# A new order of the steady loop and of both ends in a window-attention and LoRA kernel

## The chip, the cores and the metric

The kernel runs on one core of a Trainium2 chip. The metric is the device time of one execution in microseconds (us), as the median of several runs; lower is better. The core has five engines, each with a queue of its own that it works off in order: PE (matmul, with its weight loads shown as PEld), DVE (vector), ACT (scalar, activation functions), POOL (GpSimd) and SP (here it only issues DMAs). An instruction that has to wait for another engine holds up all that stand behind it in its own queue.

## The reference

The input x has 32 sequences of 512 tokens with 256 features, in float32. For each sequence:

```python
x = x + attn(layernorm(x), wq, wk, wv, wo, q_norm_w, k_norm_w)
x = x + ffn(layernorm(x), weight, gate_w, lora_U, lora_V)
# attn: 16 query heads, 4 key/value heads of 64; rmsnorm on q and k per head;
#   a query sees itself and the 127 tokens before it; softmax; then y @ wo.T
# ffn: gate = softmax(xt @ gate_w.T) over 8 experts; base = xt @ weight.T;
#   t = xt @ lora_U (rank 16); out = base + (1/16) * sum_e gate_e * (t_e @ lora_V_e)
```

## The kernel before

The tokens are cut into tiles of 128, four to a sequence, so N = 128 tiles in all; t is the place of a tile in its sequence. Each tile goes through the same stages, each a small method of the class `Tile`:

- `ln1_stats`, `ln1_eps`, `ln1_rs`, `ln1_neg`: mean and variance of x and the factor 1/sqrt(var + eps) (DVE, ACT, POOL, ACT). `trx` transposes x on DVE (L390).
- `kv_pe` (L398) and `q_pe(0)`, `q_pe(1)` (L413): matmuls to k and v, and to two halves of q. `kv_copy`, `ksq`, `q_copy`, `qsq` read the results on ACT (L404 to L426), `vdiff` reads v on DVE.
- `ksum`, `qsum` (DVE), `q_eps` (ACT), `pow` (POOL, L319), `kn`, `qn` (POOL): the norm of q and k. `trk`, `trq` transpose them in 32x32 blocks on DVE; `move` (L353) lets SP issue 16 DMAs that bring the blocks to their places, together with blocks of the probabilities and of h for other tiles; `kT_copy` reads the keys from there on ACT.
- `s_pe(0)` to `s_pe(3)` (L529): scores of 32 queries each. `s_merge` (L540), `nmaxs` (L545) on DVE, `exps` (L556) on ACT: mask, row maximum, and exponential with its sum, 4 activations for each j. `prob_den`, `prob` (DVE, POOL), `tr` (DVE): division and transposition.
- `pick` (POOL, L599): the part of the probabilities that belongs to the other half of the window. `y_pe` (L627): probabilities times v; its second half, with `other` and `vd`, exists only for t > 0. `y_copy` (ACT, L648), `o_pe` (L654), `o_add` (DVE).
- `ln2_stats`, `ln2_eps`, `ln2_rs`, `trh`, `hT_copy`, `f_pe` (L700), `gmax`, `gexp`, `gmul`, `uT_pe` (L731), `uT_copy`, `lora_pe` (L738), `store`, `put`: the second norm and the feed-forward part, and the result's DMA.

For the first tile of a sequence (t = 0) the first of its score matmuls are narrower (32 to 128 columns instead of 160), `y_pe` has no second half, and `vdiff`, `pick` and `ln1_neg` do nothing; but `s_merge` has a memset more (L539).

The order of the instructions on all five engines is written out by hand, with no scheduler behind it: `slot(i)` is the body of the steady loop and calls each stage once, for the tile that it has reached by then (`at(i - 3).s_pe(0)` is the score stage of the tile three behind i). The calls of one engine make up its queue, in the order in which they stand. The tables `FIRST` and `LAST` are the same kind of list for the first tiles and for the last ones; an entry `q_pe.1:0` is `q_pe(1)` of tile 0, `s_pe.3:-1` is `s_pe(3)` of the last tile.

The results of matmuls lie in PSUM. Four banks, B0 to B3, are shared by all stages except the scores; S0 holds s(0) and s(2), S1 holds s(1) and s(3). A matmul group can begin only when all readers of the previous content of its bank are done. `BANK` says which stage uses which bank in the loop, and `PLACES` gives exceptions, by stage and tile, for the two ends. In SBUF each kind of tile has a fixed number of buffers (`BUFS`), used in turn.

Of the kernel before, what the change touches and what calls it, by code (L numbers as in the profile page):

```python
# [30 lines left out]
def tile_window_attn_lora_ffn(  # L31
# [47 lines left out]
    N = B * NT  # L79
# [28 lines left out]
    for tag, products in {  # L108
        "B0": "tq0 y1 uT",
        "B1": "cqa q0 tq1 y0 o",  # L110
# [9 lines left out]
        ("ckv", 0): "B3",  # L120
        ("cqa", 0): "B2",
        ("cqb", 0): "B0",
        ("q0", 0): "B2",
        ("kv", 0): "B1",
        ("q0", 1): "B3",
        ("q1", 0): "B3",
        ("q0", 2): "B0",
        ("kv", 1): "B0",
        ("cf", 0): "B1",
        ("tq0", 0): "B2",  # L130
        ("tk", 0): "B3",
        ("kv", 2): "B3",
        ("tk", 1): "B0",
        ("tq0", 1): "B3",
        ("tq1", 1): "B3",
        ("q0", 3): "B0",
        ("kv", 3): "B1",
        ("tq0", 2): "B1",
        ("tq1", 2): "B2",
        ("tk", 2): "B1",  # L140
        ("q1", 4): "B0",
        ("q0", 5): "B0",
        ("kv", 5): "B3",
        ("kv", 6): "B0",
        ("y0", 0): "B0",
        ("y1", 0): "B3",
        ("q1", 6): "B3",
        ("y0", 1): "B0",
        ("y1", 1): "B3",
        ("o", 0): "B3",  # L150
        ("o", 1): "B0",
        ("y0", 2): "B3",
        ("y0", 3): "B0",
        ("y1", 3): "B3",
        ("o", 2): "B3",
# [12 lines left out]
        ("y1", -4): "B2",
        ("o", -4): "B3",
        ("f", -7): "B2",  # L170
        ("y0", -3): "B0",
        ("y1", -3): "B3",
        ("hT", -4): "B0",
        ("y0", -2): "B2",
        ("y1", -2): "B1",
        ("uT", -6): "B1",
        ("o", -2): "B2",
        ("hT", -3): "B0",
        ("f", -5): "B1",
        ("y0", -1): "B2",  # L180
        ("y1", -1): "B3",
        ("uT", -5): "B2",
        ("o", -1): "B0",
        ("f", -4): "B0",
        ("uT", -4): "B1",
        ("uT", -3): "B1",
        ("f", -2): "B0",
        ("uT", -2): "B3",
        ("f", -1): "B2",
        ("uT", -1): "B1",  # L190
# [577 lines left out]
    def slot(i):  # L768
        at(i).ln1_stats()
        at(i - 1).q_pe(0)  # L770
        at(i - 11).uT_copy()
        at(i).trx()
        at(i - 4).tr(0)
        at(i).ln1_eps()
        at(i - 1).q_copy(1)
# [181 lines left out]
    with tc.manual_schedule(engines={mybir.EngineType.PE, mybir.EngineType.Activation, mybir.EngineType.DVE, mybir.EngineType.Pool, mybir.EngineType.SP}):  # L957
        in_order(FIRST, 0)
        for i in range(12, N - 1 + 1):
            slot(i)  # L960
# [49 lines left out]
```

## Time and profile before

| what | value |
|---|---|
| median of 3 runs | 2089.67 us (2089.59 to 2089.72) |
| the profiled execution | 2090.21 us |
| its span, first to last instruction | 2088.5 us |
| PE busy | 2071.2 us, 99% |
| DVE busy | 1778.1 us, 85% |
| POOL busy | 1670.9 us, 80% |
| ACT busy | 1530.5 us, 73% |
| granted clock of PE | full over the whole span |
| first matmul starts at | 5.42 us |
| matmuls of wq and x, and of wo | 462.6 us busy (L413), 475.3 us (L654) |
| exponentials on ACT | 720.5 us (L556) |
| DMA | 138 GB/s mean |

The page gives one execution on the chip. A row of PE's timeline gives the start of a group of like matmuls, the time until the modelled end of its last one, the line, the operands and how many instructions it has; each matmul in float32 of the program is two instructions there, a transposition is one. Because the ends overlap with the next group, the distance between two starts is what a group costs. A bracket at the end of a row gives the idle time before it and what ended it.

### The profile page before, as it was taken

Reading aid. Unit: us, or ns where it says so; the run is one execution under the profiler, and the core shown is the slowest. Engines: PE = TensorE matmul, PEld = TensorE weight load, DVE = VectorE, ACT = ScalarE, POOL = GpSimd, SP = SyncE. Lnnn points to the kernel's source line nnn. Section 1 sums busy time; section 2 is a strip of 40 time slices with the busy share of each in tenths; the row PEclk is TensorE's granted clock in tenths of the full one; section 3 lists DMA queues with packets and bytes.
Section 4 is the critical chain, followed back from the end, with each engine's and each line's share of the span. In section 5 each row is a group of like instructions: output and inputs, shape, how many; then the busy total and the mean of one; then the engine's idle time right before and its main releaser. Section 6 shows DMA issues by size and latency. Waiting matters only on the chain.

```text
span 2088.5 us, 43160 instructions
## 1 busy us (share of the span) xinstructions
PE 2071.2 (99%) x12214; PEld 1282.8 (61%) x12214; DVE 1778.1 (85%) x4546; ACT 1530.5 (73%) x6247; POOL 1670.9 (80%) x1291
## 2 busy tenths in 40 slices
PE   8999999999999999999999999999999999999999
PEld 4556666666666666666666666666666666666665
DVE  6988888888888888888888888888898888888884
ACT  6877777777777777777777777777777777777773
POOL 6988778877788788888877887778878888887773
PEclk9999999999999999999999999999999999999999
DMA  5665666566656666665666656665656566656653
GB/s 116 143 154 137 140 144 143 132 140 143 144 133 142 141 140 138 142 144 137 137 142 140 146 134 140 142 146 132 143 136 148 132 143 144 139 135 140 142 130 86
DMA packets 272989, 288.79 MB, mean 138 GB/s; under 512 B 172273, under 2 KB 206705, under 8 KB 272753
## 3 DMA queue, kind: packets, MB, share of 16 engines
q1 hardware_dynamic: 272208, 284.47, 59.6%
q8 instruction: 100, 1.64, 0.4%
q10 hardware_dynamic: 544, 1.57, 0.2%
q14 instruction: 137, 1.11, 0.2%
HBM read 36.71 MB, written 16.78 MB: 26 GB/s over the span
## 4 chain that ended last, share of the span: by engine, by line
PE 89%; ACT 6%; SPq 2%; DVE 1%; DMA 1%; issue 0%; DVEq 0%; ACTq 0%
PE o_ps L654 22%; PE q_ps L413 20%; PE s_ps L529 14%; PE y_ps L627 13%; PE kv_ps L398 11%; PE f_ps L700 6%; ACT ex L556 4%; PE f_ps L738 3%; SPq L353 1%; ACT kv L404 1%; PE uT_ps L731 1%; ACT ksq L408 1%; SPq L238 0%; DVE nmax L545 0%; DMA pT<-tr 0%
## 5 line engine op out<-in xcount | busy, mean ns | idle before, releaser
L556 ACT ACTIVATE ex<-s_ps,nmax 128x128 f32<-128x128 f32 x2048 | 720.5, 387 | 28.5 <-DVE nmax L545 22.3
L319 POOL TENSOR_TENSOR rs<-ss_eps,minus_half 128x20 f32<-128x20 f32 x128 | 453.1, 3539 | 167.1 <-ACT ss_eps L441 165.8
L568 POOL TENSOR_TENSOR ex<-ex,rden 128x1024 f32<-128x1024 f32 x256 | 485.4, 1896 | 96.8 <-DVE rden L564 95.3
L654 PE MATMUL o_ps<-wo_sb,yT 128*128 128x256 f32 x2048 | 475.3, 385 | 0.3 <-ACT yT L648 0.3
L556 ACT ACTIVATION_READ_ACCUMULATOR ex<-s_ps,nmax 128x1 f32 x2048 | 465.9, 228 | 0.0
L413 PE MATMUL q_ps<-wq_sb,xT 128*128 128x512 f32 x1024 | 462.6, 593 | 0.1
L654 PEld LDWEIGHTS o_ps<-wo_sb,yT 128*128 128x128 f32 x2048 | 379.1, 190 | 68.8 <-ACT yT L648 10.6
L545 DVE TENSOR_REDUCE nmax<-s_ps 128x4 f32<-128x512 f32 x512 | 348.6, 681 | 13.0
L529 PE MATMUL s_ps<-kT,pT 64*128 64x160 f32 (+4 forms) x4000 | 335.4, 304 | 3.9 <-ACT ex L556 0.9
L529 PEld LDWEIGHTS s_ps<-kT,pT 64*128 64x128 f32 x4000 | 271.1, 186 | 104.5 <-ACT ex L556 47.0
L599 POOL TENSOR_SCALAR_AFFINE_SELECT other<-pT 64x512 f32<-64x512 f32 x384 | 289.8, 755 | 21.3 <-DMA pT<-tr 5.9
L413 PEld LDWEIGHTS q_ps<-wq_sb,xT 128*128 128x128 f32 x1024 | 184.5, 190 | 192.2 <-issue 173.8
L404 ACT ACTIVATE kv<-kv_ps,ln_rs_a 128x512 f32<-128x512 f32 x128 | 88.3, 690 | 265.0 <-PE kv_ps L398 265.0
L398 PE MATMUL kv_ps<-wkv_sb,xT 128*128 128x512 f32 x512 | 253.5, 617 | 0.6 <-DVE xT L390 0.5
L627 PE MATMUL y_ps<-pT,kv 128*64 128x256 f32 x2048 | 249.3, 385 | 0.0
L458 POOL TENSOR_TENSOR qn<-q,rs 128x1024 f32<-128x1024 f32 x128 | 243.4, 1902 | 0.2
L579 DVE STREAM_TRANSPOSE tr<-ex 128x512 f32<-128x512 f32 (+3 forms) x512 | 240.3, 487 | 2.8 <-DMA pT<-tr 1.1
L421 ACT ACTIVATE q<-q_ps,ln_rs_a 128x512 f32<-128x512 f32 x256 | 176.0, 688 | 51.5 <-PE q_ps L413 50.3
L627 PEld LDWEIGHTS y_ps<-pT,kv 128*64 128x64 f32 x2048 | 135.5, 136 | 125.9 <-ACT ss_eps L441 61.4
L540 DVE COPY_PREDICATED s_ps<-over,s_ps 128x128 f32<-128x128 int32 x512 | 148.4, 290 | 75.4 <-PE s_ps L529 70.8
L700 PE MATMUL f_ps<-wf_sb,hT 128*128 128x392 f32 x512 | 190.1, 494 | 0.1
L426 ACT ACTIVATE qsq<-q_ps,ln_rs_a 128x512 f32<-128x512 f32 x256 | 175.0, 684 | 2.0 <-PE q_ps L413 1.2
(85 smaller groups left out, 2538.3 us busy)
## 6 DMA issues: line engine op xcount, KB each, us to landing
pT<-tr SPq DMA_DIRECT2D x1936, 112.0 KB, 2.3
xb<-in_x_dram SPq DMA_DIRECT2D x256, 64.0 KB, 2.3
x<-in_x_dram SPq DMA_DIRECT2D x128, 128.0 KB, 2.4
out_dram<-res SPq DMA_DIRECT2D x128, 128.0 KB, 2.0
pT<-tr SPq DMA_DIRECT2D x64, 104.0 KB, 2.2
pT<-tr SPq DMA_DIRECT2D x48, 72.0 KB, 2.1
wq_sb<-in_wq_dram ACTq DMA_DIRECT2D x1, 1024.0 KB, 7.4
wo_sb<-in_wo_dram SPq DMA_DIRECT2D x1, 1024.0 KB, 6.5
```

Source lines behind the costliest of these rows:

```text
L319: nc.gpsimd.tensor_tensor(o, v, minus_half[:, : o.shape[-1]], ALU.pow)
L398: nc.tensor.matmul(ps, self.xT[:, c, :], wkv_sb[:, c, :], start=(c == 0), stop=(c == ND - 1))
L413: nc.tensor.matmul(ps, self.xT[:, c, :], wq_sb[:, c, gp * 512 : (gp + 1) * 512], start=(c == 0), stop=(c == ND - 1),)
L458: nc.gpsimd.tensor_tensor(self.q_n.rearrange("p (g d) -> p g d", d=HD), self.q.rearrange("p g (h d) -> p (g h) d", d=HD), self.rs[:, :NH]. ...
L529: nc.tensor.matmul(ps[:, half, gp, o0:n], qT[rows, gp * P : (gp + 1) * P], self.s.kT[rows, gp, k0 + o0 : k0 + n], start=True, stop=True,)
L545: nc.vector.tensor_reduce(self.nmax[j], ps[:, :, :, :P], AX.X, ALU.max, negate=True)
L556: nc.scalar.activation(self.ex[e][:, c, gp, half], ps[:, gp, half, :P], AF.Exp, bias=self.nmax[j][:, gp, half : half + 1], accum_out=self. ...
L568: nc.gpsimd.tensor_tensor(ex, ex, self.rden[e].rearrange("p c g a -> p (c g a)").unsqueeze(2).to_broadcast([P, 8, P]), ALU.mult,)
L599: nc.gpsimd.affine_select(out=self.other[gp][rows].rearrange("p h (c a q) -> p h c a q", c=2, a=2), in_=fr.rearrange("p h (c a q) -> p h c ...
L627: nc.tensor.matmul(ps[e][half * HD : (half + 1) * HD, gp * 4 * H : (gp + 1) * 4 * H], v[:, v0 : v0 + HD], w.rearrange("p h (c a q) -> p a ...
L654: nc.tensor.matmul(ps[:, :D], self.yT[:, c].rearrange("p e t -> p (e t)"), wo_sb[:, c, :], start=(c == 0), stop=(c == NCH - 1),)
L700: nc.tensor.matmul(ps[:, : UG + D], self.hT[:, c, :], wf_sb[:, c, :], start=(c == 0), stop=(c == ND - 1),)
```

## The change

The change rewrites the order and nothing else: the same stages run for the same tiles. It has four parts.

- `slot(i)` has a new order of its calls, and the stages are spread over more tiles: `kv_pe` and `trx` now work on tile i-2 (before: i), `q_pe(0)` and `q_pe(1)` both on i-2 (before: i-1 and i), the scores on i-5 (before: i-3), `tr` on i-6 (before: i-4), `y_pe` on i-8 (before: i-6), `o_pe` on i-9 (before: i-7), `f_pe` on i-12 (before: i-10), `lora_pe` on i-13 (before: i-11). `load_x` and `load_blocks` are called for i+1 and i+3 (before: i+3 and i+5). On PE the order within a slot was q(0), lora, s(0), s(1), kv, f, y, s(2), s(3), o, uT, q(1); it becomes s(0), s(1), kv, lora, y, s(2), s(3), f, q(0), q(1), o, uT.
- `BANK`: o and uT exchange their banks (o to B0, uT to B1).
- `FIRST` and `LAST` are written anew, to lead into this loop and out of it; the loop begins with tile 13 instead of 12.
- `PLACES` is written anew to go with them.

The diff, with the tables cut:

```diff
@@ -106,8 +106,8 @@
 
     BANK = {}
     for tag, products in {
-        "B0": "tq0 y1 uT",
-        "B1": "cqa q0 tq1 y0 o",
+        "B0": "tq0 y1 o",
+        "B1": "cqa q0 tq1 y0 uT",
         "B2": "ckv cqb hT tk kv q1",
         "B3": "cf f",
         "S0": "s0 s2",
@@ -117,77 +117,74 @@
 
 
     PLACES = {
-        ("ckv", 0): "B3",
...
+        ("ckv", 0): "B1",
...
     }
     def slot(i):
+        at(i - 4).trq()
+        at(i - 6).tr(1)
+        at(i - 6).exps(3)
+        at(i - 2).trx()
+        at(i - 3).q_copy(1)
+        at(i - 12).ln2_eps()
+        at(i - 5).s_pe(0)
+        at(i - 3).ksum()
+        at(i - 6).prob_den(1)
+        at(i - 5).s_merge(0)
+        at(i - 5).s_pe(1)
+        at(i - 13).uT_copy()
+        at(i - 8).pick(0)
+        at(i - 5).nmaxs(0)
+        at(i - 8).pick(1)
+        at(i - 10).o_add()
+        at(i - 5).s_merge(1)
+        at(i - 5).nmaxs(1)
+        at(i - 2).kv_pe()
+        at(i - 13).lora_pe()
+        at(i - 8).y_pe()
+        at(i - 5).exps(0)
+        at(i - 5).s_pe(2)
+        at(i - 3).qsum()
+        at(i - 5).exps(1)
+        at(i - 13).store()
+        at(i - 12).ln2_rs()
+        at(i - 10).trh()
+        at(i - 6).tr(0)
+        at(i - 5).prob_den(0)
+        move(i - 7)
+        at(i - 13).put()
+        at(i - 5).s_pe(3)
+        at(i - 6).prob(1)
+        at(i - 5).s_merge(2)
+        at(i - 3).q_eps()
+        at(i - 12).hT_copy()
+        at(i - 8).y_copy(0)
+        at(i - 12).f_pe()
         at(i).ln1_stats()
-        at(i - 1).q_pe(0)
-        at(i - 11).uT_copy()
-        at(i).trx()
-        at(i - 4).tr(0)
+        at(i - 5).nmaxs(2)
+        at(i - 2).kv_copy()
+        at(i - 2).q_pe(0)
+        at(i - 1).ln1_rs()
+        at(i - 1).ln1_neg()
+        at(i - 2).ksq()
+        at(i - 8).y_copy(1)
+        at(i - 2).vdiff()
+        at(i - 2).q_pe(1)
+        at(i - 12).gmax()
+        at(i - 3).pow()
+        at(i - 5).s_merge(3)
+        at(i - 3).kn()
+        at(i - 9).o_pe()
+        at(i - 6).tr(3)
+        at(i - 5).exps(2)
+        at(i - 10).ln2_stats()
+        at(i - 3).trk()
         at(i).ln1_eps()
-        at(i - 1).q_copy(1)
-        at(i - 4).tr(1)
-        at(i).ln1_rs()
-        at(i - 11).lora_pe()
-        at(i - 1).qsq(1)
-        at(i - 4).prob_den(1)
-        at(i - 3).s_pe(0)
-        at(i - 8).ln2_stats()
-        at(i).ln1_neg()
-        at(i - 4).prob(1)
-        at(i - 11).store()
-        at(i - 1).q_copy(0)
-        at(i - 3).s_pe(1)
-        at(i - 11).put()
-        at(i - 1).qsq(0)
-        at(i - 3).s_merge(0)
-        at(i).kv_pe()
-        at(i - 3).nmaxs(0)
-        at(i - 8).ln2_eps()
-        at(i - 1).qsum()
-        at(i - 6).pick(1)
-        at(i - 10).f_pe()
-        at(i - 3).s_merge(1)
-        at(i - 3).nmaxs(1)
-        at(i).kv_copy()
-        at(i - 8).ln2_rs()
-        at(i - 4).tr(2)
-        at(i).ksq()
-        at(i - 6).y_pe()
-        at(i - 1).q_eps()
-        at(i - 3).exps(0)
-        at(i).ksum()
-        at(i - 1).pow()
-        at(i).vdiff()
-        at(i - 3).exps(1)
-        at(i - 4).tr(3)
-        at(i - 10).gmax()
-        at(i - 3).s_pe(2)
-        at(i - 6).y_copy(0)
-        at(i - 3).s_pe(3)
-        at(i - 3).prob_den(0)
-        at(i - 6).y_copy(1)
-        at(i - 3).s_merge(2)
-        at(i - 7).o_pe()
-        at(i - 10).gexp()
-        at(i - 3).nmaxs(2)
-        at(i - 1).kn()
-        at(i - 3).s_merge(3)
-        at(i - 1).qn()
-        at(i - 1).trk()
-        at(i - 3).nmaxs(3)
-        at(i - 2).kT_copy()
-        at(i - 10).gmul()
-        at(i - 3).exps(2)
-        at(i - 3).prob(0)
-        at(i - 1).trq()
-        at(i - 10).uT_pe()
-        at(i).q_pe(1)
-        at(i - 3).exps(3)
-        at(i - 7).o_add()
-        at(i - 5).pick(0)
-        move(i - 4)
-        at(i - 7).trh()
-        at(i - 9).hT_copy()
-        load_x(i + 3)
-        load_blocks(i + 5)
+        at(i - 2).qsq(0)
+        at(i - 5).nmaxs(3)
+        at(i - 12).gexp()
+        at(i - 3).qn()
+        at(i - 2).qsq(1)
+        at(i - 12).gmul()
+        at(i - 2).q_copy(0)
+        at(i - 6).tr(2)
+        at(i - 5).prob(0)
+        at(i - 4).kT_copy()
+        at(i - 12).uT_pe()
+        load_x(i + 1)
+        load_blocks(i + 3)
     FIRST = """
-        ldb:2 ldb:3 mean_kv:0 ldx:0 ln1_stats:0 ldb:0 ldb:1 mean_qa:0 ldx:1 ldx:3 mean_qb:0 sub_kv:0
-        trx:0 ldx:5 ln1_eps:0 trx:1 sub_qa:0 ln1_rs:0 kv_pe:0 kv_copy:0 q_pe.0:0 sub_qb:0 ksq:0
-        qsq.0:0 ldwo:0 q_copy.0:0 ln1_stats:1 ksum:0 ldx:4 ldx:2 ln1_eps:1 ln1_stats:2 ln1_stats:4
-        q_pe.1:0 kv_pe:1 ln1_eps:2 ln1_rs:1 trx:2 ln1_neg:0 ldb:4 ldx:6 ln1_rs:2 q_pe.1:1 ln1_eps:4
...
+        ldb:0 mean_kv:0 sub_kv:0 ldb:2 ldb:1 ldb:3 ldx:1 ldx:0 ldx:2 trx:0 mean_qa:0 ldx:4 mean_qb:0
+        kv_pe:0 sub_qa:0 ldx:3 ldx:5 ln1_stats:0 ln1_eps:0 sub_qb:0 ln1_stats:1 ln1_stats:5 trx:1
+        ln1_rs:0 kv_copy:0 ksq:0 q_pe.0:0 ln1_eps:5 ln1_stats:3 q_pe.1:0 ln1_neg:0 ln1_eps:1 qsq.0:0
+        ln1_eps:3 qsq.1:0 ln1_stats:2 ldx:7 ldb:4 ln1_rs:1 q_copy.0:0 ksum:0 vdiff:0 ln1_eps:2
+        ln1_rs:5 ldb:5 qsum:0 trx:2 ldb:7 kv_pe:1 ln1_stats:7 kv_copy:1 q_eps:0 ln1_neg:5 q_copy.1:0
...
     """
     LAST = """
...
-        uT_copy:-2 uT_pe:-1 lora_pe:-2 uT_copy:-1 put:-3 lora_pe:-1 store:-2 put:-2 store:-1 put:-1
+        uT_copy:-3 ln2_rs:-2 lora_pe:-3 gmax:-2 gexp:-1 gmul:-1 store:-3 gexp:-2 gmul:-2 uT_pe:-1
+        uT_pe:-2 uT_copy:-1 put:-3 lora_pe:-1 uT_copy:-2 lora_pe:-2 store:-1 store:-2 put:-1 put:-2
     """
         in_order(FIRST, 0)
-        for i in range(12, N - 1 + 1):
+        for i in range(13, N - 1 + 1):
             slot(i)
         in_order(LAST, N)
```

## The prediction

> **What bounds the kernel now.** I read the page first (busy shares, clock, idle time before the score matmuls), then PE's timeline over a few slots of the loop, then the waits of PE's weight loads, ACT's timeline where PE paused, and the busy time by stretch of the span. The page:
>
> ```profile
> PE 2071.2 (99%) x12214; PEld 1282.8 (61%) x12214; DVE 1778.1 (85%) x4546; ACT 1530.5 (73%) x6247; POOL 1670.9 (80%) x1291
> PEclk9999999999999999999999999999999999999999
> ```
>
> PE works for 99% of the span at full clock. That could hide waits, since the ends of matmuls are modelled, so I go by starts: how long from the start of one group of matmuls to the start of the next. PE's timeline in two neighbouring slots:
>
> ```profile
> 1000.55 1.98 PE L398 MATMUL kv_ps<-wkv_sb,xT 128*128 128x512 f32 x4
> 1002.38 1.48 PE L700 MATMUL f_ps<-wf_sb,hT 128*128 128x392 f32 x4
> 1003.78 1.95 PE L627 MATMUL y_ps<-pT,kv 128*64 128x256 f32 x16
> 1005.66 1.09 PE L627 MATMUL y_ps<-other,vd 64*64 64x256 f32 x16
> 1006.69 1.36 PE L529 MATMUL s_ps<-kT,pT 64*128 64x160 f32 x16
> 1007.97 3.72 PE L654 MATMUL o_ps<-wo_sb,yT 128*128 128x256 f32 x16
> ...
> 1016.89 1.98 PE L398 MATMUL kv_ps<-wkv_sb,xT 128*128 128x512 f32 x4
> 1018.71 1.48 PE L700 MATMUL f_ps<-wf_sb,hT 128*128 128x392 f32 x4
> 1020.12 1.95 PE L627 MATMUL y_ps<-pT,kv 128*64 128x256 f32 x16
> 1022.00 1.73 PE L529 MATMUL s_ps<-kT,pT 64*128 64x160 f32 x16
> 1023.66 3.72 PE L654 MATMUL o_ps<-wo_sb,yT 128*128 128x256 f32 x16
> ```
>
> A slot is 16.34 us (kv to kv). Groups of one kind take the same time every slot: kv 1.82, f 1.41, y 1.88 plus 1.02, s 1.29, o 3.55. One differs: in the second slot y belongs to the first tile of a sequence, has no y(other,vd), and the s group after it lasts 1.66 instead of 1.29, so PE loses 0.37 there. PE's weight loads and ACT at that spot:
>
> ```profile
> 1022.00 0.57 PEld L529 LDWEIGHTS s_ps<-kT,pT 64*128 64x128 f32 x8 [0.39 <-issue]
> 1022.91 0.57 PEld L529 LDWEIGHTS s_ps<-kT,pT 64*128 64x128 f32 x8 [0.34 <-ACT ex L556]
> ```
>
> ```profile
> 1018.91 0.69 ACT L404 ACTIVATE kv<-kv_ps,ln_rs_a 128x512 f32<-128x512 f32 x1 [2.28 <-PE kv_ps L398]
> 1019.96 0.37 ACT L556 ACTIVATE ex<-s_ps,nmax 128x128 f32<-128x128 f32 x1
> ...
> 1022.70 1.13 ACT L648 COPY yT<-y_ps 128x512 f32<-128x512 f32 x2
> ```
>
> s_pe(3) needs the bank of s_pe(1), which exps(1) frees. ACT stands idle 2.28 us for kv (kv_copy is in front of the exponentials), then exps(0) and exps(1) run from 1019.96 to 1022.70 (2.74). With y short, PE is back for the bank too early. This comes once in each sequence of four slots. By stretch:
>
> ```profile
> 0.00:196.14 196.14, 186.51 (x1014) 107.72 (x1014) 163.64 (x401) 147.56 (x581) 160.94 (x126) 1.00 0.60 137
> 196.14:1994.92 1798.78, 1795.97 (x10642) 1116.42 (x10641) 1556.63 (x3976) 1335.03 (x5461) 1460.49 (x1121) 1.00 0.61 140
> 1994.92:2088.46 93.54, 88.72 (x562) 58.68 (x561) 57.85 (x169) 47.91 (x207) 49.49 (x46) 1.00 0.46 111
> ```
>
> The middle is 28 whole sequences: 1798.78 / 28 = 64.24 each, of which 0.37 is that wait. The rest is PE's own work, which no order of the same matmuls removes.
>
> **The change part by part.** No instruction is added or removed: both built programs hold 6190 matmuls with the same columns. Durations below are from the profiled execution, 2090.21 us (span 2088.5 and 1.7 around it), which is 0.5 above the median 2089.67.
>
> *Changes of tiling.* The group costs show a price for changing PE's tile size. lora's two matmuls would be 2 x 0.216 = 0.43 in a run of equal ones (o: 3.45 for 16); before s they take 0.52. kv's four take 1.82 after s, where q's eight in a row take 3.43, so four 1.72. So 0.1 on leaving a tiling and up to 0.1 on entering, 0.15 to 0.2 per change. Both loops have six changes a slot: full to s, s to full, full to y, y to y(other), y(other) to s, s to full. Over the whole program the lists count 746 before and 750 after; the four more are in the ends: 4 x 0.18 = +0.7.
>
> *PE's order in a slot.* New: s(0,1), kv, lora, y, s(2,3), f, q(0), q(1), o, uT. Same groups, same sum: 1.29 + 1.82 + 0.53 + 1.88 + 1.02 + 1.29 + 1.42 + 3.43 + 3.45 + 0.21 = 16.34. So nothing from PE itself; only waits can differ.
>
> *The wait on exps(1).* Time from the slot's s(0). Old order: from the end of s(1), kv, f and a short y give 5.1 until s(2), while ACT waits for kv. New order: kv, lora, short y give only 4.2, so s(2) starts at 5.5 and s(3) at 6.2. But exps(0) and exps(1) now stand in front of kv_copy. s(0) ends at 0.7; merge 0.33 and max 0.61 with 0.2 of signalling make 1.9; after o_add (0.42) and the second merge and max, exps(1) runs from 3.3 to 4.7. That is 1.5 before s(3) needs it, even with short y. The wait goes: 28 x 0.37 = -10.4.
>
> *What is late next.* I followed each engine's queue through a slot with row durations, in us from s(0).
> - DVE: 14.1 of work in 16.3. It waits about 1.6 for s(2), and is back for the next s_merge(0) at 16.7; s(0) is ready at 17.2: 0.5 of slack, and behind it 1.5 on the exponentials.
> - q_pe(1) takes kv's bank (B2), freed by kv_copy, ksq and vdiff. vdiff is behind s_merge(2), ln1_stats and nmaxs(2) on DVE and ends at 9.9; q_pe(1) starts at 11.0: slack 1.0.
> - kv_pe takes q(1)'s bank, freed by q_copy(1), which has moved behind exps(3) into the next slot: 16.4 against 17.6. s(1) needs exps(3): 15.9 against 17.0. Slack 1.1 each.
> - y needs uT_copy and o_add (2.3 against 3.6); f needs store (4.8 against 7.8).
> - POOL: pow 3.54, kn 0.57, qn 1.86, two prob 1.86, two pick 1.5, two small powers: 13.8. pow starts at q_eps (4.9), prob(0) ends at 12.8, both picks of the next y by 15.8, 6 before that y's second half.
> - SP: move's 16 transfers issue in 10.1 (timeline at 1011.44) and land 2.3 later. trq is now at the slot's start and frees them at -1.0; they have landed at 11.4, kT_copy reads them at 14.0, pick at 12.8. put waits behind them for store, long done. load_x runs one tile ahead of ln1_stats instead of three, still some 10 us.
>
> All positive, so I cost these at nothing; the nearest is 0.5.
>
> *The start.* Before, DVE's first work is ln1_stats(0), idle 7.11 for x; the subtraction on wkv stands behind it, and kv_pe(0) starts at 13.50 with 0.49 idle. After, that subtraction and trx(0) come first, and the x load no longer stands among the block loads on SP. kv_pe(0) can follow the mean matmuls (11.13 + 1.72): -0.65.
>
> *The first 13 tiles.* The page of before leaves there, in its own order: 1.94 where uT(1) waits for u (145.12), 0.87 at 72 to 74 and 0.54 at 58.37 for the exponentials, 0.4 each at 38.88, 127.19 and 186.85, 0.37 at 69.78: about 5. The new order has other pauses, which this trace can't show. The range runs from none (-5) to twice as many (+5). POOL is the limit there (19.4 to 19.6 of 20 us busy between 75 and 115); the two lists hold the same POOL work up to qn of tile 9 and the new one starts it some 1.5 earlier: pow(0) stood at 22.54; now kv(0) at 12.9, both q until 18.0, square 18.9, qsum 20.1, kv_copy(1) 20.7 and q_eps give 21.0. So I take half: -2.5.
>
> *The end.* Before, from the start of the last o (2074.42) to the end is 14.0 against 8.6 of PE work. The new list leaves 10.6 behind it: the last f ends at 9.0, gate and u take 2.2 (lg, gmax, exponential, reciprocal, product and signals), uT and its copy 1.0, so the last lora starts at about 12.3, and from there to the end it was 3.8: 16.1. Both lose 5.5: 0, with 2 either way.
>
> Sum against the profiled execution: 2090.2 - 10.4 + 0.7 - 0.65 - 2.5 = 2077.4; as a median, 0.5 lower: **2077**.
>
> A rule that speaks against this: the Trainium skill, Perfetto Trace Analysis, "Identifying the Most-Contended Engine", says matmul occupancy is no measure of PE's closeness to its limit and goes by weight-load time, here 61%; DVE with 85% would then be most contended, and an order that gives DVE the same work would gain nothing, about 2090. The equal group times above, slot after slot, speak for PE being full.
>
> **The rivals.**
> - *The ends give it back.* Thirteen lead tiles and a longer tail leave more work in hand-ordered stretches. Against it: POOL's earlier start. At the far bound (+5 there, +2 at the tail) the time is 2077 + 7.5 + 2 = 2086.5; half of that, 2082, is the likelier.
> - *The wait moves.* s(3) no longer waits, but in the short slot q_pe(1) or s(1) does, by the same 0.37 a sequence: 2077 + 10.4 = 2087.4, within 0.2% of before together with small losses at the ends. For it: the short slot takes 1.0 from everyone; against it: the slacks there stay at 1.0 and more, since DVE's wait for s(2) shortens too.
> - *A wait in every slot (slower).* vdiff is late for q_pe(1): DVE is the fullest queue behind PE (85%), and one late instruction in it delays all behind. The walk leaves 1.0. The gain of 12.7 over about 115 slots is 0.11 a slot, so it decides once DVE is 1.1 later than I make it; at 1.3 late the loss is 0.3 x 115 = 34, and the time 2111.
> - *Nothing changes* would need PE's loss to lie elsewhere than in that s group; the timeline leaves no room for it.
>
> **How the numbers follow.** Forecast case (loop free of waits, ends as summed) 0.70, own range 2072 to 2081: the starts' -5 to +5 around -2.5, and 2 at the tail, not both at their worst. Ends give back 0.15, 2081 to 2086.5. Wait moves 0.06. Wait in every slot 0.09. The measurement tells 0.2% (4.2 us) from no change, so faster means under 2085.5: 0.70 + 0.14 + 0.02 = 0.86; same 0.05; slower 0.09. The 80% range leaves out the worst of the slower cases and the far ends: 2072 to 2086.
>
> **What would show it.** Right: s groups of 1.29 (1.04 to 1.09 in a first tile) in every slot, a sequence of 63.87 us, no idle of PE's loads on ACT's exponentials beyond the 0.1 of a tiling change, kv_pe(0) near 12.9. Wrong: a q group over 3.44 with PE waiting for DVE's vd, a kv group waiting for ACT's q, a sequence of 64.2 or more, or over 5 us of pauses before the third sequence's end.

## The result and the profile after

| | median, us | runs |
|---|---|---|
| before | 2090.09 | 6 runs, 2089.59 to 2091.36 |
| after | 2076.16 | 6 runs, 2075.46 to 2076.89 |
| ratio | 0.9932 | 95% interval 0.9920 to 0.9945 |

The changed kernel is faster by 0.7%, 13.9 us. The forecast was 2077, in a range of 2072 to 2086. The profiled span went from 2088.5 to 2074.6. The kernels below ran on different chips, each beside before, whose medians there were 2089.56 to 2090.40; differences between two of them of less than about 1 us are not read as effects.

Line numbers of the changed kernel are 3 lower than before: s is L526, kv L395, q L410, y L624, the exponentials L553, the row maximum L542.

The page of the new kernel, busy times first, then its chain of waits by engine, then two of its groups:

```profile
PE 2062.1 (99%) x12214; PEld 1292.2 (62%) x12214; DVE 1730.8 (83%) x4546; ACT 1521.3 (73%) x6247; POOL 1669.2 (80%) x1291
PE 97%; SPq 1%; DVE 1%; DMA 0%; ACT 0%; issue 0%; ACTq 0%
...
L553 ACT ACTIVATE ex<-s_ps,nmax 128x128 f32<-128x128 f32 x2048 | 723.7, 374 | 262.7 <-DVE nmax L542 253.8
...
L537 DVE COPY_PREDICATED s_ps<-over,s_ps 128x128 f32<-128x128 int32 x512 | 149.2, 292 | 194.6 <-PE s_ps L526 189.8
```

The same line of the chain in the page of before:

```profile
PE 89%; ACT 6%; SPq 2%; DVE 1%; DMA 1%; issue 0%; DVEq 0%; ACTq 0%
```

ACT has left the chain: 6% before, 0% after. The other engines now wait where PE waited before. ACT stands 253.8 us for DVE's row maxima, DVE 189.8 us for the scores of PE. That idle time costs nothing, as the chain says.

PE's timeline of the new kernel over one slot, the short one, in which y belongs to the first tile of a sequence:

```profile
1007.46 1.36 PE L526 MATMUL s_ps<-kT,pT 64*128 64x160 f32 x16
1008.75 1.98 PE L395 MATMUL kv_ps<-wkv_sb,xT 128*128 128x512 f32 x4
1010.57 0.59 PE L735 MATMUL f_ps<-wv_sb,uT 128*128 128x256 f32 x2
1011.09 1.95 PE L624 MATMUL y_ps<-pT,kv 128*64 128x256 f32 x16
1012.97 1.36 PE L526 MATMUL s_ps<-kT,pT 64*128 64x160 f32 x16
1014.26 1.58 PE L697 MATMUL f_ps<-wf_sb,hT 128*128 128x392 f32 x4
```

The second s group takes 1.29 from start to start, like the first. Before it took 1.66 in this slot. ACT's exponentials of the same slot, of which the first group of eight is in question:

```profile
1009.46 0.37 ACT L553 ACTIVATE ex<-s_ps,nmax 128x128 f32<-128x128 f32 x1 [1.57 <-DVE nmax L542]
...
1012.22 0.26 ACT L438 ACTIVATE ss_eps<-ss 128x20 f32<-128x20 f32 x1
1012.32 0.44 ACT L687 COPY hT<-pT 128x256 f32<-128x256 f32 x1
1012.65 0.60 ACT L645 COPY yT<-y_ps 128x512 f32<-128x512 f32 x1
1013.14 0.70 ACT L401 ACTIVATE kv<-kv_ps,ln_rs_a 128x512 f32<-128x512 f32 x1
```

ACT goes on to its next instruction at 1012.22, 4.76 after the slot's s(0); s(3) starts at 1013.62 (1012.97 and half of 1.29), 6.15 after it. kv_copy now comes after the exponentials, at 1013.14.

Busy times by stretch: up to the first scores of tile 12, from there to the first scores of tile 124, and the rest, as in the table of before:

```profile
0.00:192.57 192.57, 185.77 (x1012) 108.35 (x1012) 160.38 (x398) 147.82 (x579) 159.90 (x124) 1.00 0.61 139
192.57:1977.53 1784.96, 1784.96 (x10625) 1121.41 (x10624) 1509.92 (x3969) 1324.77 (x5454) 1457.18 (x1119) 1.00 0.62 141
1977.53:2074.63 97.10, 91.36 (x582) 62.45 (x580) 60.46 (x181) 48.71 (x215) 52.07 (x50) 0.99 0.46 111
```

A sequence in the steady loop takes 63.87 (958.90 to 1022.77) against 64.24. (The mean over the 28 is 63.75, because the last of them runs into the new tail's order and takes 60.70.) The three stretches do not hold equal work in the two kernels: the new lists have 1.1 us more of PE's work before the first mark and 2.8 more behind the second. So I compare PE's pauses, that is, the start of a group less the summed price of all groups ahead of it (start-to-start prices, the same for both kernels). What a matmul takes beyond its price, as the first ones of the program do, counts as a pause too:

| PE's pauses, us | before | after | difference |
|---|---|---|---|
| until the first kv matmuls | 8.35 | 7.97 | -0.4 |
| from there to the first scores of tile 12 | 6.38 | 2.06 | -4.3 |
| the 28 sequences of the loop | 13.31 | 2.65 | -10.7 |
| the rest | 7.30 | 8.05 | +0.75 |
| PE's own work (four more changes of tiling) | 2053.12 | 2053.90 | +0.8 |
| sum, the span | 2088.46 | 2074.63 | -13.8 |

### The profile page after: what moved, and what is told of

Read it like the earlier page. It is cut to its first block, busy times and chain, and to the rows that moved or that the text cites. A ratio compares the mean times of both kernels' runs of the same rounds, so it can differ in the third digit from the quotient of the medians.

```text
span 2074.6 us, 43742 instructions
## 1 busy us (share of the span) xinstructions
PE 2062.1 (99%) x12214; PEld 1292.2 (62%) x12214; DVE 1730.8 (83%) x4546; ACT 1521.3 (73%) x6247; POOL 1669.2 (80%) x1291
## 3 DMA queue, kind: packets, MB, share of 16 engines
q14 instruction: 137, 1.12, 0.2%
## 4 chain that ended last, share of the span: by engine, by line
PE 97%; SPq 1%; DVE 1%; DMA 0%; ACT 0%; issue 0%; ACTq 0%
PE o_ps L651 21%; PE q_ps L410 20%; PE y_ps L624 16%; PE s_ps L526 15%; PE kv_ps L395 11%; PE f_ps L697 9%; PE f_ps L735 3%; SPq L350 1%; PE uT_ps L728 1%; DMA wkv_sb<-in_wkv_dram 0%; PE ckv_ps_mean L299 0%; DVE nmax L542 0%; PE cqa_ps_mean L299 0%; ACT ex L553 0%; DVE ss L432 0%
## 5 line engine op out<-in xcount | busy, mean ns | idle before, releaser
L553 ACT ACTIVATE ex<-s_ps,nmax 128x128 f32<-128x128 f32 x2048 | 723.7, 374 | 262.7 <-DVE nmax L542 253.8
L651 PE MATMUL o_ps<-wo_sb,yT 128*128 128x256 f32 x2048 | 463.4, 379 | 0.0
L410 PE MATMUL q_ps<-wq_sb,xT 128*128 128x512 f32 x1024 | 462.3, 593 | 0.8 <-DVE vd L613 0.8
L651 PEld LDWEIGHTS o_ps<-wo_sb,yT 128*128 128x128 f32 x2048 | 388.5, 190 | 104.1 <-issue 29.2
L553 ACT ACTIVATION_READ_ACCUMULATOR ex<-s_ps,nmax 128x1 f32 x2048 | 435.0, 213 | 0.0
L542 DVE TENSOR_REDUCE nmax<-s_ps 128x4 f32<-128x512 f32 x512 | 344.9, 674 | 9.0
L410 PEld LDWEIGHTS q_ps<-wq_sb,xT 128*128 128x128 f32 x1024 | 193.6, 190 | 218.1 <-issue 163.9
L526 PE MATMUL s_ps<-kT,pT 64*128 64x160 f32 (+4 forms) x4000 | 327.1, 302 | 0.4 <-ACT ex L553 0.4
L526 PEld LDWEIGHTS s_ps<-kT,pT 64*128 64x128 f32 x4000 | 270.3, 187 | 88.1 <-issue 58.0
L537 DVE COPY_PREDICATED s_ps<-over,s_ps 128x128 f32<-128x128 int32 x512 | 149.2, 292 | 194.6 <-PE s_ps L526 189.8
L395 PE MATMUL kv_ps<-wkv_sb,xT 128*128 128x512 f32 x512 | 253.1, 617 | 0.0
L576 DVE STREAM_TRANSPOSE tr<-ex 128x384 f32<-128x384 f32 (+3 forms) x512 | 248.4, 486 | 3.3 <-DMA pT<-tr 1.9
L624 PE MATMUL y_ps<-pT,kv 128*64 128x256 f32 x2048 | 249.3, 385 | 0.0
L645 ACT COPY yT<-y_ps 128x512 f32<-128x512 f32 x256 | 151.6, 594 | 93.8 <-PE y_ps L624 93.8
L697 PE MATMUL f_ps<-wf_sb,hT 128*128 128x392 f32 x512 | 201.7, 517 | 0.0
L624 PEld LDWEIGHTS y_ps<-pT,kv 128*64 128x64 f32 x2048 | 135.7, 136 | 98.0 <-issue 40.3
L316 POOL TENSOR_TENSOR ln_rs_f<-ln_v_f,minus_half 128x1 f32<-128x1 f32 x128 | 70.0, 548 | 138.5 <-ACT ln_v_f L328 117.4
```

The source lines that it names most:

```text
L316: nc.gpsimd.tensor_tensor(o, v, minus_half[:, : o.shape[-1]], ALU.pow)
L395: nc.tensor.matmul(ps, self.xT[:, c, :], wkv_sb[:, c, :], start=(c == 0), stop=(c == ND - 1))
L410: nc.tensor.matmul(ps, self.xT[:, c, :], wq_sb[:, c, gp * 512 : (gp + 1) * 512], start=(c == 0), stop=(c == ND - 1),)
L526: nc.tensor.matmul(ps[:, half, gp, o0:n], qT[rows, gp * P : (gp + 1) * P], self.s.kT[rows, gp, k0 + o0 : k0 + n], start=True, stop=True,)
L542: nc.vector.tensor_reduce(self.nmax[j], ps[:, :, :, :P], AX.X, ALU.max, negate=True)
L553: nc.scalar.activation(self.ex[e][:, c, gp, half], ps[:, gp, half, :P], AF.Exp, bias=self.nmax[j][:, gp, half : half + 1], accum_out=self. ...
```

## The experiments

The theory, as predicted: the loop gains because exps(0) and exps(1) have come in front of kv_copy on ACT's queue, so that the bank S1 is free when s(3) comes; the rest is a shorter head, which POOL limits, and an unchanged tail. The rivals: the wait has merely moved; DVE is so near its limit that vdiff delays q(1); the loop gains by something else, as its matmul order or banks.

### One reorder undone, and the same reorder alone

In the new loop, kv_copy and ksq back in front of the exponentials:

```diff
+        at(i - 2).kv_copy()
+        at(i - 2).ksq()
         at(i - 5).exps(0)
 ...
-        at(i - 2).kv_copy()
 ...
-        at(i - 2).ksq()
```

> The changed kernel with one part undone: in the loop, kv_copy and ksq stand in front of exps(0) again. Theory (the gain of the loop comes from the exponentials standing in front of kv_copy): from the slot's s(0), kv is done for ACT at 3.3, kv_copy and ksq take 0.94, exps(0) runs until 5.6 and exps(1) until 7.0. In the slot with a short y, s(3) could start at 6.2 and starts at 7.1: its s group grows from 1.29 to about 2.2. In the other slots s(3) is due at 7.2, so 0 to 0.1. A sequence 64.8 instead of 63.87, the time about 2102. Rival (the place of the exponentials does not matter, the gain lies in the ends or in the spreading over more tiles): 2076, sequence 63.87.

Measured: 2124.60 (4 runs), ratio to before 1.0166 (1.0152 to 1.0180). PE's timeline of this kernel in the short slot:

```profile
1032.88 1.95 PE L624 MATMUL y_ps<-pT,kv 128*64 128x256 f32 x16
1035.06 0.81 PE L526 MATMUL s_ps<-kT,pT 64*128 64x160 f32 x8 [0.23 <-ACT ex L553]
1036.45 0.81 PE L526 MATMUL s_ps<-kT,pT 64*128 64x160 f32 x8 [0.58 <-ACT ex L553]
1037.20 1.58 PE L697 MATMUL f_ps<-wf_sb,hT 128*128 128x392 f32 x4
```

From y to f takes 4.32, against 3.17 in the new kernel: 1.15 lost here, before s(2) and before s(3), and both waits name the exponentials. The direction is the expected one, the size is not: 48 us instead of 26. The other three slots of a sequence, which I had taken for free, lose 0.1 to 0.2 each (their s(2) takes 0.67 to 0.73 where it took 0.52 or 0.65, their s(3) 0.64 to 0.74 where it took 0.57 or 0.64). In sum 1.64 a sequence (65.39 against 63.75, means of the same 28), times 28 is 46.

In the kernel before, the same reorder alone (with ksum, which reads the result of ksq, moved behind it on DVE), everything else as it was:

```diff
-        at(i).kv_copy()
 ...
-        at(i).ksq()
 ...
-        at(i).ksum()
 ...
         at(i - 3).exps(1)
+        at(i).kv_copy()
+        at(i).ksq()
 ...
         at(i - 3).prob_den(0)
+        at(i).ksum()
```

> The kernel before with this part alone: kv_copy and ksq behind exps(1) in its loop, and ksum, which reads ksq, behind prob_den(0); nothing else moved, ends as they were. Theory: exps(0) and exps(1) end about 1.2 before s(3) needs the bank in the slot with a short y, all s groups are 1.29 there, a sequence 63.87 instead of 64.24, 28 times 0.37 gone: about 2079.5, head and tail as before. Rival (the loop's gain needs the new lags and the new order of PE): 2090, sequence 64.24; or a new wait, because ksum and then pow come later: above 2090.

Measured: 2079.57 (5 runs), ratio 0.9951 (0.9937 to 0.9965). PE's timeline of this kernel in the short slot, in the order of before:

```profile
1013.81 1.48 PE L700 MATMUL f_ps<-wf_sb,hT 128*128 128x392 f32 x4
1015.22 1.95 PE L627 MATMUL y_ps<-pT,kv 128*64 128x256 f32 x16
1017.10 1.36 PE L529 MATMUL s_ps<-kT,pT 64*128 64x160 f32 x16
1018.38 3.72 PE L654 MATMUL o_ps<-wo_sb,yT 128*128 128x256 f32 x16
```

The s group takes 1.28 instead of 1.66. Two calls moved on ACT and one on DVE give 10.5 of the 13.9 us. So the new order of matmuls, the new delays and the banks of the loop were not needed for the loop's gain; what this kernel lacks against the new one, 3.4, lies in the ends, since a sequence of its loop takes 63.87 as well.

### How much room DVE has left

In the new loop, a reduction that nobody needs in front of vdiff, first of 512 columns (0.59 from its start to that of the next instruction), then of 1024 and 512 (1.72):

```diff
+        def spend(self, c):
+            junk = small.tile([P, 4 * c], F32, tag="junk", bufs=2, name=f"junk_{self.n}_{c}")
+            nc.vector.tensor_reduce(
+                junk, wo_sb[:, :c].rearrange("p c (h d) -> p (c h) d", d=HD), AX.X, ALU.add
+            )
 ...
+        at(i - 2).spend(4)     # only in the second kernel
+        at(i - 2).spend(2)
         at(i - 2).vdiff()
```

> The changed kernel with one more reduction on DVE in each slot of the loop, 512 columns, some 0.6 us, right before vdiff; its result is not used. Theory (vdiff has 1.0 to 1.3 to spare before q(1) needs its bank, and DVE waits 1.0 for s(0) at the slot's start): loop unchanged at 63.87 a sequence, 2076. Rival (DVE, 83% busy, is nearly the limit of the loop): 0.5 to 0.6 in each of 115 slots, 2134 to 2145.

Measured: 2077.49 (one run). The 28 sequences of this kernel:

```profile
192.98:1978.61 1785.63, 1785.63 (x10625) 1119.07 (x10624) 1567.73 (x4081) 1323.59 (x5454) 1455.55 (x1119) 1.00 0.62 141
```

They take 63.77 each (63.75 without the reduction); the span is 1.1 longer, of which 0.4 is a later first kv group (13.54 against 13.12) and 0.6 the loop.

> The new kernel with two reductions more on DVE in every slot of the loop (1024 and 512 columns, together about 1.7 us) ahead of vdiff. It prices the rival that I put at 2111, a wait in every slot because vdiff is late for q(1). The walk left 1.0 there and the trace of the new kernel shows 1.27 in a short slot: at 1.7 the second q group starts 0.4 to 0.65 late in every one of the 115 slots, and DVE comes to 15.8 of 16 us of work, so that s_merge(0) of the next slot is late too: 2076 + 46 to 75 = 2122 to 2151. If it stays under 2085, the slack is larger than either reading says.

Measured: 2149.7 (one run). DVE and PE at one such place:

```profile
1000.78 1.80 DVE L619 TENSOR_REDUCE junk<-wo_sb 128x16 f32<-128x1024 f32 x2
1002.50 0.47 DVE L610 SCALAR_TENSOR_TENSOR vd<-kv_ps,ln_rs_a,kv 64x256 f32<-64x256 f32 x1
1002.98 0.49 DVE L613 SCALAR_TENSOR_TENSOR vd<-kv_ps,minus_rs,kv 64x256 f32<-64x256 f32 x1
```

```profile
1000.82 1.88 PE L410 MATMUL q_ps<-wq_sb,xT 128*128 128x512 f32 x4
1003.62 1.95 PE L410 MATMUL q_ps<-wq_sb,xT 128*128 128x512 f32 x4 [0.92 <-DVE vd L613]
```

q(1) waits for vdiff, just as the slower rival had it. From q(0) to q(1) the four slots of a sequence take 2.80, 1.72, 2.32 and 2.32 instead of 1.72: nothing in the slot whose vdiff does nothing (first tile of a sequence), 0.60 in two, 1.08 in the one where the scores are those of a first tile and s_merge has its memset. So the slack is 1.72 - 0.60 = 1.12 in the common slots and 1.72 - 1.08 = 0.64 in that one. 0.59 more costs next to nothing (0.02 a sequence), 1.72 more costs 73 us.

### What limits the head

In the new kernel, one more pow on POOL (3.54), for nobody, ahead of the first tile's:

```diff
+        def pow_twice(self):
+            junk = small.tile([P, NH + KV], F32, tag="junk", bufs=1, name="junk")
+            rsqrt(junk, self.ss_eps)
 ...
-        ... ksq:1 pow:0 q_pe.1:1 qsq.1:1
+        ... ksq:1 pow_twice:0 pow:0 q_pe.1:1 qsq.1:1
```

> The new kernel with one more pow of 3.54 us on POOL ahead of the first tile's pow, its result used by nobody. Theory: POOL limits the first 13 tiles, so its earlier start is what shortened them; then the 3.54 comes through nearly whole: the score group of tile 3's successor sequences starts later, the one that I use as a mark (first scores of the fourth tile, at 192.57 in the new kernel) at about 196, and the time is 2076.2 + 3.5 = 2079.7. Rival: the new head is shorter because of its order on PE, and POOL has slack in it; then PE's other work covers most of the 3.54, the mark moves by less than 1.5 and the time stays under 2077.7.

Measured: 2079.48 (4 runs), ratio 0.9948 (0.9931 to 0.9964). The first scores of tile 12, the mark that the expectation calls those of the fourth tile, come at 195.61. From the first kv group to there it takes 182.69 against 179.45: 3.24 of the 3.54 come through. Most of it is paid at one place, PE's timeline there, in this kernel and in the new one:

```profile
24.93 1.48 PE L299 MATMUL cf_ps_mean<-wf_sb,mean_m 128*128 128x392 f32 x4
28.70 0.44 PE L482 MATMUL tk_ps<-ident,kn 128*128 128x128 f32 x2 [2.29 <-POOL kn L450]
```

```profile
25.14 1.48 PE L299 MATMUL cf_ps_mean<-wf_sb,mean_m 128*128 128x392 f32 x4
26.45 0.38 PE L478 MATMUL tk_ps<-ident,kn 128*128 128x128 f32 x2
```

The theory holds at this place: PE had hardly any other work to do under a later POOL. At which other places of the head POOL limits it was not tested.

In the new kernel, the old order at the very start, x of tile 0 and its statistics ahead of the subtraction on wkv:

```diff
-        ldb:0 mean_kv:0 sub_kv:0 ldb:2 ldb:1 ldb:3 ldx:1 ldx:0 ldx:2 trx:0 mean_qa:0 ldx:4 mean_qb:0
-        kv_pe:0 sub_qa:0 ldx:3 ldx:5 ln1_stats:0 ln1_eps:0 sub_qb:0 ...
+        ldb:0 mean_kv:0 ldx:0 ln1_stats:0 sub_kv:0 ldb:2 ldb:1 ldb:3 ldx:1 ldx:2 trx:0 mean_qa:0 ldx:4 mean_qb:0
+        kv_pe:0 sub_qa:0 ldx:3 ldx:5 ln1_eps:0 sub_qb:0 ...
```

> The new kernel with the start's old order on DVE and SP alone: the load of x for tile 0 and its statistics ahead of the subtraction on wkv. Theory: the first kv matmuls wait for that subtraction again, about 0.4 to 0.6 later (13.5 to 13.7 against 13.12), and the rest of the head, which PE fills, carries it to the end: 2076.6. Rival: the first pow on POOL is what the head waits for, and it needs the statistics early; then the delay is made up before the fourth tile and the time is 2076.2 or below.

Measured: 2076.71 (4 runs), ratio 0.9934 (0.9920 to 0.9949). This does not tell the two theories apart. PE's timeline at the start, where the groups ckv, cqa and cqb take the means that are subtracted from the weights, and then PE's weight loads:

```profile
5.32 3.75 PE L299 MATMUL ckv_ps_mean<-wkv_sb,mean_m 128*128 128x512 f32 x4 [5.32 <-DMA wkv_sb<-in_wkv_dram]
8.88 2.91 PE L299 MATMUL cqa_ps_mean<-wq_sb,mean_m 128*128 128x512 f32 x4
11.63 1.88 PE L299 MATMUL cqb_ps_mean<-wq_sb,mean_m 128*128 128x512 f32 x4
13.35 1.89 PE L395 MATMUL kv_ps<-wkv_sb,xT 128*128 128x512 f32 x4
```

```profile
8.88 0.50 PEld L299 LDWEIGHTS cqa_ps_mean<-wq_sb,mean_m 128*128 128x128 f32 x2 [1.39 <-DMA wq_sb<-in_wq_dram]
9.90 0.34 PEld L299 LDWEIGHTS cqa_ps_mean<-wq_sb,mean_m 128*128 128x128 f32 x1 [0.52 <-issue]
11.20 0.19 PEld L299 LDWEIGHTS cqb_ps_mean<-wq_sb,mean_m 128*128 128x128 f32 x1 [0.24 <-issue]
13.25 0.30 PEld L395 LDWEIGHTS kv_ps<-wkv_sb,xT 128*128 128x128 f32 x2 [0.58 <-DVE xT L387]
```

kv follows the mean matmuls with no wait of PE, 1.72 after the last group's start, although DVE subtracts later; x, issued earlier here than before, was in at 9.77 (11.02 before). It is the mean matmuls that come late: ckv takes 3.56 from start to start and cqa 2.75, where such a group takes 1.72 later on. Their matmuls run at half the later rate: they start 0.85 apart (0.43 later), and a weight load takes 0.34 (0.19 later), until about 10.8 here. The late DMA of wq, for which the first load of cqa waits, explains 0.2 of it at most. kv's own weight load waits for xT until 13.25, so DVE was ready only 0.1 before PE: had the mean matmuls been as early as in the kernel `e7_y_beside_s` below, whose first kv group starts at 12.12, the old order would have cost about 1.2 (an estimate from these two traces). What the new order is worth at the start depends on how long the slow matmuls last. In all traces taken with the new start order, the first kv group starts between 12.10 and 13.54; with the old one at 13.50 and 13.69. A scatter of 1.4 between executions is larger than the term that I was after.

### Can the loop go below PE's present sum?

The changes of tiling are part of PE's sum. With y right behind s(0) and s(1), one change of the six falls away. In two slots of four (those in which neither the scores nor y belong to a first tile) the new loop got PE's order s(0), s(1), y, s(2), s(3), kv, lora, q(0), f, q(1), o, uT (`e7_y_beside_s`), with uT_copy and o_add earlier to free the banks, and other calls moved to fit:

```diff
+    def slot_y(i):
 ...
+        at(i - 5).s_pe(1)
 ...
+        at(i - 8).y_pe()
+        at(i - 5).exps(0)
+        at(i - 5).s_pe(2)
+        at(i - 3).qsum()
+        at(i - 5).exps(1)
+        at(i - 5).s_pe(3)
 ...
-            slot(i)
+            (slot_y if i % NT > 1 else slot)(i)
```

> A trial to go further: in two of four slots (where neither y nor s belongs to a first tile) PE does s(0), s(1), y, s(2), s(3), kv, lora, q(0), f, q(1), o, uT, which has five changes of tile size instead of six; o_add comes ahead of s_merge(0) and store behind the third merge to fit. If a change costs 0.15 to 0.2, as the group times of before say, these slots take 16.14 to 16.18 instead of 16.34, a sequence 63.5, and the time is 2064 to 2067. Against it: s(3) comes 4.9 after s(0) and exps(1) ends at 4.7, so 0.2 to spare; if it is late by 0.3 in each of these slots the gain is gone and the time is 2076 to 2082.

Measured: 2078.02 (4 runs), ratio 0.9942 (0.9929 to 0.9956): no gain over the new order. PE's timeline in such a slot:

```profile
978.52 1.57 PE L526 MATMUL s_ps<-kT,pT 64*128 64x160 f32 x16
980.02 1.98 PE L395 MATMUL kv_ps<-wkv_sb,xT 128*128 128x512 f32 x4
981.84 0.59 PE L735 MATMUL f_ps<-wv_sb,uT 128*128 128x256 f32 x2
982.27 1.88 PE L410 MATMUL q_ps<-wq_sb,xT 128*128 128x512 f32 x4
983.99 1.48 PE L697 MATMUL f_ps<-wf_sb,hT 128*128 128x392 f32 x4
985.31 1.88 PE L410 MATMUL q_ps<-wq_sb,xT 128*128 128x512 f32 x4
```

The saving is there, lora takes 0.43 instead of 0.52 and f 1.32 instead of 1.42; so the prediction's "no order of the same matmuls removes" PE's own work was too strong. But the s group takes 1.50 instead of 1.29: s(2) 0.76 instead of 0.65 and s(3) 0.74 instead of 0.64. Waits of PE's weight loads in the loop of this kernel:

```profile
PEld s_ps L526 <- ACT ex L553: 11.1, 56, 0.5
```

56 waits are one for each such slot. In the new kernel that line does not exist in the loop. Three more kernels asked what stands behind this wait.

First (`e9_y_beside_s_dve`), in those slots, two instructions of DVE moved from in front of s_merge(0) to behind the second maximum:

```diff
-        at(i - 2).trx()
 ...
-        at(i - 3).ksum()
 ...
         at(i - 5).nmaxs(1)
+        at(i - 2).trx()
+        at(i - 3).ksum()
```

> The kernel of e7_y_beside_s with two more moves on DVE in the slots that have its order: the transposition of xT (0.40) and the sum over ksq (0.38) go from in front of o_add to behind the second row maximum. In e7 those slots lost 0.2 where s(3) waits for the exponentials of s(1) (56 times, 11.1 us by the waits of PE's weight loads), which start with DVE's first maximum; s_merge(0) began there 0.15 to 0.2 after s(0) had ended, behind o_add. Theory: e7's saving of one tiling change a slot is real and the wait ate it. With s_merge(0) 0.14 earlier the wait shrinks from about 0.11 to nothing and the 0.1 behind it goes too: two slots of four at 0.2, 28 sequences, 11 us: 2066 to 2068. Rival: the s groups of 0.76 and 0.74 are the price of that order on PE and no wait: then nothing changes, 2077 to 2078.

Measured: 2078.19 (5 runs), ratio 0.9944 (0.9931 to 0.9958), s(2) still 0.76. The expectation failed: s_merge(0) starts 0.86 after s(0) in both kernels. DVE now waits there for s(0) itself (0.44 idle); the two instructions had stood in time that DVE would have waited anyway.

Second (`e11_first_max_in_two`, which keeps these moves), the first row maximum in two reductions of half the columns, so that the exponentials might begin sooner:

```diff
-        at(i - 5).nmaxs(0)
+        at(i - 5).nmaxs_by_pair(0)    # for gp in range(GP): tensor_reduce(nmax[:, gp], ps[:, gp, :, :P], ...)
```

> The kernel of e9_y_beside_s_dve, where the row maximum over s(0) is taken in two reductions of half the columns in the slots with y beside s, so that the first exponentials can start after the first half. In e9 nothing moved: s_merge(0) waits for s(0) itself (0.44 idle), so the chain s(0), merge 0.33, maximum 0.61, eight exponentials 2.76 is what s(3) waits for, 0.11 too long. Theory: the first half takes about 0.4, exps(0) starts 0.25 earlier, exps(1) 0.15 to 0.25 earlier (its own maximum comes 0.1 later), the wait on s(3) and the 0.1 behind it go: 28 x 2 x 0.2 = 11, so 2066 to 2068. Rival: 0.76 and 0.74 are PE's own price of s right behind y(other) in a run of short tiles: 2077 to 2079 again. A third: two reductions cost DVE more than the half saves, and s(3) waits longer: over 2080.

Measured: 2081.37 (5 runs), ratio 0.9961 (0.9947 to 0.9974). s(2) takes 0.82 to 0.83, 0.07 more than in the kernel before this one.

Third (`e12_max_in_two_tiles`), the two halves in tiles of their own:

```diff
-            self.nmax[j] = small.tile([P, GP, 2], F32, tag="nmax", bufs=8, ...)
+            self.nmax[j] = []
             for gp in range(GP):
-                nc.vector.tensor_reduce(self.nmax[j][:, gp], ps[:, gp, :, :P], AX.X, ALU.max, negate=True)
+                m = small.tile([P, 1, 2], F32, tag=f"nmax{gp}", bufs=3, ...)
+                nc.vector.tensor_reduce(m, ps[:, gp : gp + 1, :, :P], AX.X, ALU.max, negate=True)
+                self.nmax[j].append(m)
```

> The kernel of e11_first_max_in_two, where the two halves of the maximum over s(0) go to two tiles of their own, so that the first exponentials need to wait for the first half alone. In e11 they waited for both: the two halves took 0.76 where one reduction took 0.69, and the s(2) groups went from 0.76 to 0.83: the chain behind s(0) sets them, and they are no price of PE. Theory: exps(0) now starts 0.25 to 0.3 earlier than in e9, s(3) is no longer late, the groups return to 0.65 and 0.64, a sequence takes 63.4 instead of 63.8, and the time is 2066 to 2068. Rival: the exponentials of s(1) become the limit (their own maximum is 0.1 later than in e9) and a wait of 0.1 remains: 2072 to 2078.

Measured: 2081.65 (5 runs), ratio 0.9963 (0.9949 to 0.9977). DVE and ACT of this kernel:

```profile
977.02 0.29 DVE L537 COPY_PREDICATED s_ps<-over,s_ps 128x128 f32<-128x128 int32 x1 [0.44 <-PE s_ps L526]
977.35 0.75 DVE L549 TENSOR_REDUCE nmax<-s_ps 128x2 f32<-128x256 f32 x2
```

```profile
978.22 0.37 ACT L561 ACTIVATE ex<-s_ps,nmax 128x128 f32<-128x128 f32 x1 [1.64 <-DVE nmax L549]
```

One half takes 0.42, so a start at about 977.9 was possible; the exponentials start at 978.22, after both. The program that is built from this text holds a single signal after the second half, and the first exponential waits for that. So the idea of an earlier start was not tried; what the two kernels do show is the chain itself. It grew by 0.07 (0.76 for two halves where one reduction took 0.69) and s(2) grew by 0.07. The wait on s(3) is the length of the chain s(0), merge, maximum, eight exponentials, and no price of PE for this order. The chain needs 0.1 more room than y gives.

### Two pauses of the ends

Last, the new kernel with two of the pauses left in its ends taken out by order: the scaling of wv (0.72 on DVE) from in front of vdiff of tile 7 to a place where DVE idles, and y of tile 125 in front of lora of tile 120 (`e14_two_pauses`). Beside it, on the same chip, the new kernel unchanged (`e15_after_again`).

```diff
-        ksq:7 wv_scale:0 tr.0:2 ...
+        ksq:7 tr.0:2 ...
 ...
-        ... ksq:10 s_merge.0:7 ...
+        ... ksq:10 wv_scale:0 s_merge.0:7 ...
 ...
-        ... lora_pe:-8 tr.2:-1 store:-8 tr.3:-1 y_pe:-3 y_copy.0:-3 ...
+        ... tr.2:-1 tr.3:-1 y_pe:-3 lora_pe:-8 store:-8 y_copy.0:-3 ...
```

> The new kernel with two of the pauses that its trace still shows taken away by order alone. In the head, the one scaling of wv (0.72 on DVE, needed only by the first lora) stands in front of vdiff of tile 7, for which q(1) of that tile waits 0.87 at 71.39; it goes to 152, where DVE idles 1.71. In the tail, lora of tile 120 stands right behind the copy of its uT and waits 0.58; y of tile 125 goes in front of it. Theory: PE's pauses there are whole losses, as those of the loop were, so 0.72 (up to 1.4, if the pause of 0.65 behind it goes too) and 0.5: 1.2 to 1.9 below the new kernel run beside it, 2074.3 to 2075. Rival: ends are not additive, the next wait takes the time: no difference above 0.4.

> The new kernel unchanged, as the measure on the same chip for e14_two_pauses, whose difference of one or two microseconds is smaller than what separates two calls. Both theories expect 2075.5 to 2077; the first kv matmuls between 12.1 and 13.5, as in the runs so far, and from there to the first scores of tile 12 179.45.

Measured: 2076.47 (5 runs) with the edits, 2076.13 (5 runs) without: no difference. In the traces the head's edit works, from the first kv group to the first scores of tile 12 it takes 178.96 against 179.59 (the pause at q(1) of tile 7 is 0.38 instead of 0.88). The tail's edit does not: lora's pause of 0.57 is gone, but y in its new place waits 0.48 and the next f 0.52: from the first scores of tile 124 to the end it takes 97.58 against 97.09. So 0.6 gained, 0.5 lost, and the first kv group, at 13.34 against 12.75, covers what is left. None of the kernels here beats the changed one.

Not tried: the new loop with the old banks of o and uT. There o would need the bank B1 right behind q(1), while q_copy(0), which reads q(0) from it, stands behind o in the new order; q_copy(0) would have to move as well.

## Why the prediction was right

It was right in the time (2077 forecast, 2076.16 measured), in its mechanism for the loop and, but for two terms, in its parts:

| term | predicted | measured |
|---|---|---|
| the wait on exps(1), 28 times | -10.4 | -10.7 |
| four more changes of tiling | +0.7 | +0.8 |
| the start | -0.65 | -0.4 |
| the first 13 tiles | -2.5 | -4.3 |
| the end | 0, 2 either way | +0.75 |
| sum | -12.85 | -13.8 |

That the sum is within 1 us is in part luck: the first 13 tiles gave 1.8 more than was summed, and the start, the end and the changes of tiling together took 1.1 of that back.

**The loop.** The step that carried the forecast, one wait of 0.37 in one slot of four, is confirmed from both sides: the reorder alone brings 10.5 in the old kernel, and its undoing costs 48 in the new one. No wait took its place. Of the walk through the short slot, exps(1) ended at 4.76 (walked 4.7), vdiff left 1.27 for q(1) (walked 1.0), DVE idled 1.02 before the next s_merge(0) (walked 0.5).

**The slower rival.** Its mechanism is real, as the two reductions on DVE show, and its point was placed well for the common slots (1.12 of slack measured, 1.0 walked). But I had walked only the short slot. The least slack, 0.64, is in the slot whose scores are those of a first tile, where s_merge has a memset more. There the wait begins once DVE is 0.7 later, not 1.1.

**The start.** The term is of the right sign, but one trace can't carry it. The step "kv_pe(0) can follow the mean matmuls (11.13 + 1.72)" holds: kv comes 1.71 to 1.75 after the start of the last of them in every trace with the new start; but the 11.13 was a property of that one execution. In the trace after, that group starts at 11.40, since cqa, whose slow matmuls lasted longer there, took 2.49 instead of 2.17.

**The first 13 tiles** is the term that was mis-sized: -4.3 against -2.5. I took half of the old pauses for want of a way to see the new ones. In fact nearly all of the old ones went, and two new ones came (0.87 at 71.39 and 0.65 at 79.42). The largest old one alone was 1.94, where uT of tile 1 waited for u. That POOL limits this part was right: of an added 3.54 on POOL 3.24 came through, so the 1.4 by which the first pow came earlier (21.12 against 22.54) would be worth about 1.3, if an earlier POOL helps as much as a later one hurts. That, and how the rest of 4.3 divides, was not measured.

**The end** lost 0.75 within the bounds given.

**The rule cited against.** The Trainium skill, Perfetto Trace Analysis, "Identifying the Most-Contended Engine", read by its weight-load share alone, would have made DVE the bound and, so I took it, the gain nothing. With PEld at 62% in the new kernel, PE's groups stand back to back and DVE takes 0.59 more in every slot for next to nothing. The measurement decides against that reading. The section names a second measure beside it, the share of peak arithmetic, which was not worked out for this kernel.

## What to carry to other kernels

Where one engine's groups take the same time in every round but for one, look at that one: the odd 0.37 us, and what stood in front of its releaser in the releaser's queue, was three quarters of the gain, and three moved calls would have had it. A walk through the queues gives slacks to some tenths of a us, but walk every kind of round, not only the tightest for the engine you watch. And before moving an instruction to shorten a chain, look whether the engine would have waited there anyway.

## What was not expected of the hardware

- A wait of PE ahead of s(3) costs about 0.1 more than itself: s(3) then takes 0.74 instead of 0.64 (0.64 instead of 0.57 where its scores are narrow), in the kernels with kv first and with y beside s alike. A lone s group between two changes of tiling takes 0.74 too (67.16 in the new kernel, y next at 67.90), so the 0.1 may be what PE pays at any fresh start of such a group; no run tests that. The 0.37 of before has the same shape: by the weight loads shown there, s(3) starts 0.91 after s(2) instead of 0.65, and o starts 0.75 after s(3) instead of 0.64.
- Giving up one change of tiling showed up as 0.09 at lora and 0.10 at f, so 0.1 a side, as the prediction had read it from group times.
- The start is not reproducible to better than 1.4 us: 12.10 to 13.54 for the first kv group in eleven traces with the new start. The first matmul varies less, 5.28 to 5.76. What varies is how long the mean matmuls behind it run at half the later rate (0.85 from start to start instead of 0.43): for 3.3 us from the first one on in the trace with the earliest kv group, for 5.9 in the one with the latest. The granted clock in these stretches is shown as full. What ends the slow phase no run here shows.
